# Two rows per partition, 64x64 tiles and a ScalarE that copies: a batched product with residual rebuilt around 8 KB runs

## The chip, the cores and the metric

The kernel runs on one core of one Trainium2 chip. The metric is the device time of one execution in microseconds (us), as the median of the runs. Before the change it is 322.92 us, the median of 3 runs between 322.70 and 323.04.

## The reference

128 batch items `x[b]` of 128 rows by 1024 float32 (64 MB in all), an index `subjects[b]` of 0 to 7 for each, and eight 128x128 weights:

```
w = weights[subjects]                        # (128, 128, 128)
out = x + einsum('bct,bcd->bdt', x, w)       # out[b] = x[b] + w[b].T @ x[b]
```

All of x is read once and all of the output, of the same size, is written once: 134 MB through the DMA engines, in float32.

## The kernel before, in words

The 128 items are worked in 32 turns of four (`NT = 32`, `G = H = 2`). A turn's four items lie in one of 12 slots of an SBUF buffer, `x_all`, with a row of an item on each partition: 4 KB in one run per item and partition. The product is added to the item in place, and the slot is stored from there.

- **Loads** (L134, issued at L223 to L224): ScalarE does nothing else. It issues 128 loads of 512 KB. Up to the twelfth turn nothing but the queue holds them up (slot 11 first waits until the weights that pass through it are sorted); after that the load of turn i waits until the store of turn i - 12 has landed (L222). In DRAM a load is read as 32 rows of 16 KB (`ROWS = 4`), in SBUF it is written as 128 runs of 4 KB.
- **Weights** (L192 to L239): one load on SP's queue, two transposes and twelve copies on VectorE and four copies on GpSimd put the eight matrices into `w_all`. Before each half turn VectorE copies two of them, picked by the index, into the `ws` buffers (`place`, L163).
- **Products** (`multiply`, L168): TensorE makes two matmuls of 128x128 by 512 columns for an item, eight in a turn, four for each half of the eight PSUM banks. The three matmuls at L200 on zeros come ahead of all.
- **Adds** (`add`, L183): VectorE adds half a turn, 128 x 2048, from PSUM to the items in their slot.
- **Stores** (L142, issued at L247 to L255): SP waits for the adds and stores a turn (2 MB), or two turns (4 MB) at a time for the last twelve. From the eighth turn on it holds a store back by four turns (`BEHIND`), and ceases to do so for the last eight. In SBUF a store reads runs of 16 KB (32 KB in the last six turns), in DRAM it writes rows of 4 KB.

The engines run from their own instruction streams, with semaphores between them. GpSimd only turns landed loads into a count that TensorE waits on (L240 to L245).

Of the kernel before, what the change touches and what calls it, by code (L numbers as in the profile page):

```python
# [25 lines left out]
F32 = mybir.dt.float32  # L26
I32 = mybir.dt.int32
ALU = mybir.AluOpType


G = 2
H = 2

N = 512

SLOTS = 12

P_SLOTS = 2

BEHIND = 4  # L40

EARLY = 8
LAST = 8

PAIR = 2
WHOLE = 6

DMA = 16

SORTED = 18  # L50

IDLE = 3

ROWS = 4

ALIGN = 4096
QUEUES = {mybir.EngineType.SP: "qSPDynamicHW", mybir.EngineType.Activation: "qActDynamicHW"}
# [23 lines left out]
def kernel(  # L81
# [7 lines left out]
    nc = tc.nc  # L89
    B, C, T = x.shape  # L90
    S, _, D = weights.shape
    NT = B // (G * H)

    def sbuf(name, *shape, dtype=F32):
        return ctx.enter_context(nc.sbuf_tensor(name, list(shape), dtype)).ap()


    room = -(nc.sbuf_base + -nc.sbuf_base % 32) % ALIGN
    if room:
        sbuf("room", C, room // 4)  # L100
    x_all = sbuf("x_all", C, SLOTS * H * G * T)
    xs = [
        x_all[:, i * H * G * T : (i + 1) * H * G * T].rearrange("c (q t) -> c q t", t=T)
        for i in range(SLOTS)
    ]
    w_all = sbuf("w_all", C, S, D)
    w_raw, w_mid, w_late = (xs[SLOTS - 1][:, q, :] for q in range(3))
    ws = [sbuf(f"w{i}", C, 1, D) for i in range(H * G)]
    zeros = sbuf("zeros", C, N)
    given, near, wrap = (sbuf(name, 1, B, dtype=I32) for name in ("given", "near", "wrap"))  # L110
    index = sbuf("index", 1, B + H * G, dtype=I32)
    ps = [
        ctx.enter_context(nc.psum_tensor(f"ps{i}", [D, G, T], F32)).ap() for i in range(P_SLOTS)
    ]
# [5 lines left out]
    s_product = tc.alloc_semaphore("s_product")  # L120
    s_added = tc.alloc_semaphore("s_added")

    s_ready = tc.alloc_semaphore("s_ready")
    s_go = tc.alloc_semaphore("s_go")

    s_slot = [tc.alloc_semaphore(f"s_slot{k}") for k in range(SLOTS)]
    s_head = tc.alloc_semaphore("s_head")
    s_sort = tc.alloc_semaphore("s_sort")

    def emptied(i):  # L130
        turns = i // SLOTS
        return DMA * (H * G + 1) * turns - (DMA * G if i >= SLOTS and i % SLOTS == 0 else 0)

    def load(engine, i, q):  # L134
        transfer(
            nc,
            engine,
            xs[i % SLOTS][:, q, :],
            x[i * H * G + q].rearrange("(a r) t -> a (r t)", r=ROWS),
        ).then_inc(s_head if i * H * G + q < G else s_slot[i % SLOTS], DMA)  # L140

    def store(i, n):  # L142
        at = i % SLOTS * H * G * T
        return transfer(
            nc,
            nc.sync,
            out[i * H * G : (i + n) * H * G].rearrange("g d t -> d g t"),
            x_all[:, at : at + n * H * G * T].rearrange(
                "d (o t) -> d o t", o=1 if i >= NT - WHOLE else n
            ),  # L150
        )

    def subjects_of(i):
        _, subject = nc.values_load_multi_w_load_instructions(
            index[0:1, i] if isinstance(i, slice) else index[0:1, bass.ds(i * (H * G), H * G)],
            engines=[mybir.EngineType.DVE],
            min_val=0,
            max_val=S - 1,
            skip_runtime_bounds_check_because="the index is clamped on the chip above",
        )  # L160
        return subject

    def place(h, subject):  # L163
        for q in range(h * G, (h + 1) * G):
            copy = nc.vector.tensor_copy(ws[q], w_all[:, bass.ds(subject[q], 1), :])  # L165
        copy.then_inc(s_go, 1)

    def multiply(slot, h):  # L168
        nc.tensor.wait_ge(s_go, 1).then_inc(s_go, -1)
        nc.tensor.wait_ge(s_ready, 1).then_inc(s_ready, -1)  # L170
        for q in range(h * G, (h + 1) * G):
            for t in range(0, T, N):
                at = slot * (H * G * T) + (q * T + t)
                mm = nc.tensor.matmul(  # L174
                    ps[h][:, q % G, t : t + N],
                    ws[q][:, 0, :],
                    x_all[:, bass.ds(at, N)],
                    start=True,
                    stop=True,
                )  # L180
        mm.then_inc(s_product, 1)

    def add(slot, h):  # L183
        mine = x_all[:, bass.ds(slot * (H * G * T) + h * G * T, G * T)]
        nc.vector.wait_ge(s_product, 1).then_inc(s_product, -1)  # L185
        nc.vector.tensor_tensor(  # L186
            mine, ps[h].rearrange("d g t -> d (g t)"), mine, ALU.add
        ).then_inc(s_added, 1)

    with tc.tile_critical():  # L190

        nc.sync.dma_start(  # L192
            w_raw, weights.rearrange("s (u j) d -> (s u) (j d)", j=S)
        ).then_inc(s_wall, DMA)
        nc.sync.dma_start(given, subjects.rearrange("(o b) -> o b", o=1)).then_inc(s_given, DMA)

        nc.vector.memset(zeros, 0.0).then_inc(s_zeros, 1)  # L197
        nc.tensor.wait_ge(s_zeros, 1)
        for _ in range(IDLE):
            nc.tensor.matmul(  # L200
                ps[P_SLOTS - 1][:, G - 1, :N], zeros[:, :D], zeros, start=True, stop=True
            )

        nc.vector.wait_ge(s_wall, DMA)
        nc.vector.transpose(  # L208
            w_mid.rearrange("p (e h w j) -> p j h e w", e=S, h=4, w=4), w_raw
        ).then_inc(s_sort, 1)  # L210
        nc.vector.memset(index[:, B:], 0).then_inc(s_index, 1)  # L211
        nc.vector.wait_ge(s_given, DMA)
        nc.vector.tensor_scalar(near, given, -S, S - 1, ALU.max, ALU.min).then_inc(s_index, 1)  # L213
        nc.vector.wait_ge(s_index, 2)
        nc.vector.tensor_scalar(wrap, near, 0, S, ALU.is_lt, ALU.mult).then_inc(s_index, 1)  # L215
        nc.vector.wait_ge(s_index, 3)
        nc.vector.tensor_tensor(index[:, :B], near, wrap, ALU.add).then_inc(s_index, 1)  # L217
        for i in range(NT):
            if i == SLOTS - 1:
                nc.scalar.wait_ge(s_sort, SORTED)  # L220
            if i >= SLOTS:
                nc.scalar.wait_ge(s_slot[i % SLOTS], emptied(i))  # L222
            for q in range(H * G):  # L223
                load(nc.scalar, i, q)  # L224

        nc.vector.wait_ge(s_sort, 1)
        nc.vector.transpose(w_late, w_mid).then_inc(s_sort, 1)  # L227

        def sort(engine, o, v):
            engine.tensor_copy(  # L230
                w_all[32 * v : 32 * (v + 1), 2 * o : 2 * (o + 1), :],
                w_late[32 * o : 32 * (o + 1)].rearrange("c (e v d) -> c v e d", v=4, d=D)[:, v],
            ).then_inc(s_sort, 1)

        nc.vector.wait_ge(s_sort, 2)
        nc.gpsimd.wait_ge(s_sort, 2)
        for o in range(4):
            for v in range(4):
                sort(nc.gpsimd if v == 3 else nc.vector, o, v)  # L239
        for i in range(NT):  # L240
            if i == 0:
                nc.gpsimd.wait_ge(s_head, DMA * G).then_inc(s_ready, 1)
                nc.gpsimd.wait_ge(s_slot[0], DMA * G).then_inc(s_ready, 1)
            else:
                nc.gpsimd.wait_ge(s_slot[i % SLOTS], emptied(i) + DMA * H * G).then_inc(s_ready, H)  # L245

        for i in [*range(NT - SLOTS), *range(NT - SLOTS, NT, PAIR)]:  # L247
            n = 1 if i < NT - SLOTS else PAIR
            nc.sync.wait_ge(s_added, (i + n + (BEHIND if EARLY <= i < NT - LAST else 0)) * H)
            if i == 0:  # L250
                nc.sync.dma_start(
                    out[: H * G].rearrange("g d t -> d g t"), xs[0]
                ).then_inc(s_slot[0], DMA)
            elif i + n < NT:
                store(i, n).then_inc(s_slot[i % SLOTS], DMA)  # L255


        nc.vector.wait_ge(s_index, 4)
        nc.vector.wait_ge(s_sort, SORTED)
        subject = subjects_of(slice(0, H * G))  # L260
        for h in range(H):
            place(h, subject)
        with nc.vector.Fori(0, NT) as turn:  # L263
            subject = subjects_of(turn + 1)
            for h in range(H):
                add(turn % SLOTS, h)
                place(h, subject)
        with nc.tensor.Fori(0, NT) as turn:
            for h in range(H):
                multiply(turn % SLOTS, h)  # L270

    with tc.tile_critical() as waits:
        for i in range(NT - SLOTS, NT - PAIR, PAIR):
            nc.scalar.wait_ge(s_slot[i % SLOTS], emptied(i + SLOTS))
    last = store(NT - PAIR, PAIR)

    tc.add_manual_dep(
        last.ins,
# [31 lines left out]
```

## Time and profile before

| | |
|---|---|
| median of the runs | 322.92 us |
| span of the profiled execution (first to last instruction) | 320.9 us |
| rest of its time, taken as the median less the span | 2.0 us |
| moved by DMA | 134.76 MB in 10,803 packets, mean 420 GB/s over the span |
| busy: TensorE, weight loads, VectorE, GpSimd | 78%, 32%, 54%, 1% |
| mean granted clock of TensorE | 0.893 |

The profile gives the span of one execution and not that execution's own time, so what lies around the span is put at 2.0 us. "Share" of a DMA queue is the time that its packets took, as a share of 16 engines' time; the two data queues are q1 (SP's, stores mostly) and q10 (ScalarE's, loads). A packet is counted by the side that is read. A row of a window (`a:b`) counts what begins in it.

A float32 matmul of the program stands twice in the trace, as two weight loads and two matmuls, one behind the other: 512 rows for 256 matmuls. One such row is called a pass below.

### The profile page before, as it was taken

Reading aid. Unit: us, or ns where it says so; the run is one execution under the profiler, and the core shown is the slowest. Engines: PE = TensorE matmul, PEld = TensorE weight load, DVE = VectorE, ACT = ScalarE, POOL = GpSimd, SP = SyncE. Lnnn points to the kernel's source line nnn. Section 1 sums busy time; section 2 is a strip of 40 time slices with the busy share of each in tenths; the row PEclk is TensorE's granted clock in tenths of the full one; section 3 lists DMA queues with packets and bytes.
Section 4 is the critical chain, followed back from the end, with each engine's and each line's share of the span. In section 5 each row is a group of like instructions: output and inputs, shape, how many; then the busy total and the mean of one; then the engine's idle time right before and its main releaser. Section 6 shows DMA issues by size and latency. Waiting matters only on the chain. (4 is left out here: it accounts for less than half of the span.)

```text
span 320.9 us, 2386 instructions
## 1 busy us (share of the span) xinstructions
PE 248.9 (78%) x518; PEld 102.8 (32%) x518; DVE 172.6 (54%) x216; POOL 1.9 (1%) x8
## 2 busy tenths in 40 slices
PE   6199999999997699998498469988599957874000
PEld 2134444444433244443133224333244422331000
DVE  4636776777676167775435362675367745066000
POOL 0200000000000000000000000000000000000000
PEclk9679999999999599999789797999799989599555
DMA  7999999999999999999999999999999999999996
GB/s 294 425 425 412 426 423 432 429 423 425 425 425 425 425 424 425 425 429 425 429 435 431 427 427 429 425 425 425 425 425 425 425 425 425 427 427 455 429 445 274
DMA packets 10803, 134.76 MB, mean 420 GB/s; under 512 B 2481, under 2 KB 2482, under 8 KB 3122
## 3 DMA queue, kind: packets, MB, share of 16 engines
q1 hardware_dynamic: 4658, 67.64, 49.7%
q10 hardware_dynamic: 6144, 67.12, 49.6%
q14 instruction: 1, 0.01, 0.0%
HBM read 67.63 MB, written 67.11 MB: 420 GB/s over the span
## 5 line engine op out<-in xcount | busy, mean ns | idle before, releaser
L174 PE MATMUL ps<-x_all,w 128*128 x512 | 243.8, 635 | 42.0 <-PEq L170 34.3
L186 DVE TENSOR_TENSOR x_all<-ps,x_all 128x2048 f32 x64 | 146.7, 2292 | 117.3 <-DVEq L185 117.3
L174 PEld LDWEIGHTS ps<-x_all,w 128*128 128x128 f32 x512 | 100.9, 203 | 185.2 <-issue 184.6
L165 DVE COPY w<-w_all 128x128 f32 x132 | 23.2, 219 | 0.8 <-DVE w_all L230 0.8
L200 PE MATMUL ps<-zeros 128*128 128x512 f32 x6 | 5.2, 1033 | 1.7 <-DVE zeros L197 1.7
L230 DVE COPY w_all<-x_all 32x256 f32<-32x256 f32 x12 | 3.9, 326 | 0.4
L208 DVE STREAM_TRANSPOSE x_all<-x_all 128x1024 f32<-128x1024 f32 x1 | 2.0, 1992 | 3.1 <-DMA x_all<-in_L_cond_weights_dram 3.1
L200 PEld LDWEIGHTS ps<-zeros 128*128 128x128 f32 x6 | 1.8, 328 | 3.7 <-issue 2.1
L230 POOL COPY w_all<-x_all 32x256 f32<-32x256 f32 x4 | 1.7, 425 | 8.3 <-DVE x_all L227 8.1
L227 DVE STREAM_TRANSPOSE x_all<-x_all 128x1024 f32<-128x1024 f32 x1 | 1.2, 1225 | 0.0
L197 DVE MEMSET zeros<- 128x512 f32 x1 | 0.5, 485 | 1.0 <-SPq L190 1.0
L217 DVE CUSTOM_DVE_ANT_0 index<-near,wrap 1x256 uint16<-1x256 uint16 x1 | 0.3, 280 | 0.0
L215 DVE TENSOR_SCALAR wrap<-near 1x128 int32<-1x128 int32 x1 | 0.2, 215 | 0.0
L213 DVE TENSOR_SCALAR near<-given 1x128 int32<-1x128 int32 x1 | 0.2, 205 | 0.0
L297 POOL MEMSET const-bfloat16-1.0<- 128x1 bf16 x1 | 0.1, 100 | 0.0
L297 POOL MEMSET const-float32-0.0<- 128x1 f32 x1 | 0.1, 98 | 0.2 <-issue 0.2
L297 POOL MEMSET const-uint8-127<- 128x1 uint8 x1 | 0.1, 98 | 0.0
L297 POOL MEMSET const-float32-1.0<- 128x1 f32 x1 | 0.1, 97 | 0.0
L297 DVE BASE_LOAD x1 | 0.0, 21 | 0.1
L211 DVE MEMSET index<- 1x4 int32 x1 | 0.1, 62 | 0.0
## 6 DMA issues: line engine op xcount, KB each, us to landing
x_all<-in_x_dram ACTq DMA_DIRECT2D x128, 512.0 KB, 34.2
out_dram<-x_all SPq DMA_DIRECT2D x20, 2048.0 KB, 18.3
out_dram<-x_all SPq DMA_DIRECT2D x6, 4096.0 KB, 30.3
x_all<-in_L_cond_weights_dram SPq DMA_DIRECT2D x1, 512.0 KB, 3.7
given<-in_itok_B_dram SPq DMA_DIRECT2D x1, 0.5 KB
```

The source lines that it names most:

```text
L165: copy = nc.vector.tensor_copy(ws[q], w_all[:, bass.ds(subject[q], 1), :])
L174: mm = nc.tensor.matmul(ps[h][:, q % G, t : t + N], ws[q][:, 0, :], x_all[:, bass.ds(at, N)], start=True, stop=True,)
L186: nc.vector.tensor_tensor(mine, ps[h].rearrange("d g t -> d (g t)"), mine, ALU.add).then_inc(s_added, 1)
L197: nc.vector.memset(zeros, 0.0).then_inc(s_zeros, 1)
L200: nc.tensor.matmul(ps[P_SLOTS - 1][:, G - 1, :N], zeros[:, :D], zeros, start=True, stop=True)
L208: nc.vector.transpose(w_mid.rearrange("p (e h w j) -> p j h e w", e=S, h=4, w=4), w_raw).then_inc(s_sort, 1)
L213: nc.vector.tensor_scalar(near, given, -S, S - 1, ALU.max, ALU.min).then_inc(s_index, 1)
L215: nc.vector.tensor_scalar(wrap, near, 0, S, ALU.is_lt, ALU.mult).then_inc(s_index, 1)
L217: nc.vector.tensor_tensor(index[:, :B], near, wrap, ALU.add).then_inc(s_index, 1)
L227: nc.vector.transpose(w_late, w_mid).then_inc(s_sort, 1)
L230: engine.tensor_copy(w_all[32 * v : 32 * (v + 1), 2 * o : 2 * (o + 1), :], w_late[32 * o : 32 * (o + 1)].rearrange("c (e v d) -> c v e d", ...
L297: nc = _bacc.Bacc("TRN2", target_bir_lowering=False, num_devices=1)
```

## The change

The work is still 32 turns of four items, but:

- **Layout.** Two rows of an item lie on one partition, so an item fills 64 partitions with runs of 8 KB, and a pair of items (`H = 2`) fills 128. A turn is two such pairs (`P = 2`). Loads are 1 MB, 64 in all, read as 32 rows of 32 KB and written as 128 runs of 8 KB. Stores write runs of 8 KB.
- **Two buffers.** Input has 4 slots (`x_in`), output 8 (`x_out`), instead of 12 that serve as both.
- **Products.** An item's contraction is split into the two rows of a partition (`R = 2`, summed in PSUM), and its output rows too, so an item takes 8 matmuls of 64x64 by 512 columns: 32 in a turn, 1024 in all. The first pair of a turn uses the diagonal tiles of the array (rows and columns 0 to 63, or 64 to 127, for its items); the second pair uses the other two tiles, so that its items come out in each other's half of the partitions.
- **Residual.** Ones are added to the weights' diagonal when they are placed (`same`), so the matmul's result is the output, and only a copy out of PSUM is left. VectorE places 64x256 pieces, four in a turn, into one of two sets of buffers, for the turn after next.
- **Copies.** VectorE copies the first pair, two copies of 128x1024 in a turn. ScalarE copies the second pair, four copies of 64x1024, and puts each into the other half of the partitions (`swap`). A ScalarE copy of one element then tells SP.
- **Loads in ScalarE's loop.** ScalarE issues the first eight loads at once and the weights behind the first; the loads of turn i + 4 follow in its stream on its copies of turn i and on VectorE's signal `s_eaten`.
- **Weights.** They come in rows of 512 bytes on ScalarE's queue, are spread over the partitions by four matmuls with a 0/1 matrix (`pick`), and are copied out of PSUM by ScalarE and VectorE, one half each. Six matmuls on zeros come first.
- **Stores.** One turn each for 20 turns, then pairs of turns; none is held back.

On ScalarE's stream, the loads before stand one behind the other, with waits for slots only; `x_all` is the slot buffer, `in_x_dram` the input:

```order
L67 DMA x_all<-in_x_dram 128x1024 x44
L67 DMA x_all<-in_x_dram 128x1024 [waits s_sort]
L67 DMA x_all<-in_x_dram 128x1024 x3
L67 DMA x_all<-in_x_dram 128x1024 [waits s_slot0]
L67 DMA x_all<-in_x_dram 128x1024 x3
```

After the change the stream begins with nine loads (`in_L_cond_weights_dram` are the weights), and then goes through turns such as this one (`s_product1` comes from TensorE, `s_room1` from landed stores):

```order
L63 DMA x_in<-in_x_dram 128x2048
L63 DMA x_out<-in_L_cond_weights_dram 128x8x128
L63 DMA x_in<-in_x_dram 128x2048 x7
L231 ACT_TABLE_LOAD
L231 COPY w_all<-ps 128x8x128 [waits s_picked]
L306 UNCONDITIONAL_BRANCH
L225 ISA [waits s_room1,s_product1]
L225 COPY x_out<-ps 64x1024
```

```order
L225 ISA [waits s_product1]
L225 COPY x_out<-ps 64x1024
L225 ISA
L225 COPY x_out<-ps 64x1024
L243 ISA
L243 COPY mark<-same 1x1
L61 ISA [waits s_eaten]
L63 DMA x_in<-in_x_dram 128x2048
L61 ISA
L63 DMA x_in<-in_x_dram 128x2048
```

So the 48 loads of the first twelve turns stood ahead of any wait for a store, and now eight stand ahead of the first wait for a product.

On TensorE, the loop before has two waits in a turn, each ahead of four matmuls (`s_go` is for placed weights, `s_ready` for landed loads):

```order
L174 ISA [waits s_go,s_ready]
L174 MATMUL ps<-x_all,w 128x512
L174 ISA
L174 MATMUL ps<-x_all,w 128x512
L174 ISA
L174 MATMUL ps<-x_all,w 128x512
```

Now a turn has 32 matmuls of half the partitions, and waits besides for the banks that the copies have freed (`s_free0` from VectorE, `s_free1` from ScalarE):

```order
L202 MATMUL ps<-x_in,w 64x512 [waits s_go,s_ready,s_free0,s_free1]
L202 MATMUL ps<-x_in,w 64x512 x7
L202 MATMUL ps<-x_in,w 64x512 [waits s_free0,s_free1]
L202 MATMUL ps<-x_in,w 64x512 x23
```

Eight matmuls fill the first half of the banks, and the wait for the second half stands between them and the other 24.

The core of the diff:

```diff
+    def load(k, p, turn=None):
+        at = (k % IN * P + p) * SIZE
...
+            x_in[:, at : at + SIZE],
+            x[bass.ds(first, H)].rearrange("h (b r) t -> (h b) (r t)", r=ROWS),
+        ).then_inc(s_in[k % IN], DMA)
...
+            out[i * Q : (i + n) * Q].rearrange("(g h) (a r) t -> (h a) g (r t)", h=H, r=R),
+            x_out[:, at : at + n * P * SIZE].rearrange("a (o f) -> a o f", o=1),
...
+        for b in range(BANKS):
+            if b < BANKS // 2:
+                for p in range(P):
+                    nc.tensor.wait_ge(s_free[p], 1 + p).then_inc(s_free[p], -1 - p)
+            for r in range(R):
+                for p in reversed(range(P)):
+                    for h in range(H):
+                        bank = b * 2 % BANKS + (b * 2 // BANKS + h) % 2
+                        e, t = divmod(bank * N, T)
+                        rows = slice(h * A, (h + 1) * A)
+                        cols = slice((h ^ p) * A, ((h ^ p) + 1) * A)
+                        at = (i % IN * P + p) * SIZE + r * T + t
+                        mm = nc.tensor.matmul(
+                            ps[p][cols, bank],
+                            ws[i % 2][p][rows, 0, r * D + e * A : r * D + (e + 1) * A],
+                            x_in[rows, at : at + N],
...
+                        if r == R - 1 and b >= BANKS // 2:
+                            mm.then_inc(s_product[p], 1)
...
+    def swap(slot, half, h):
+        at, banks = half_of(slot, half)
+        return nc.scalar.copy(
+            x_out[h * A : (h + 1) * A, bass.ds(at + SIZE, T)],
+            ps[1][(1 - h) * A : (2 - h) * A, banks].rearrange("d b n -> d (b n)"),
+        )
...
+    def take(i):
+        slot = i % OUT if isinstance(i, int) else i
+        nc.scalar.wait_ge(s_room[1], 1).then_inc(s_room[1], -1)
+        for half in range(2):
+            nc.scalar.wait_ge(s_product[1], H).then_inc(s_product[1], -H)
+            for h in range(H):
+                swap(slot, half, h).then_inc(s_free[1], 1)
+        nc.scalar.copy(mark[:, bass.ds(slot, 1)], same[:1, 0, :1]).then_inc(s_added[1], 1)
...
+        with nc.scalar.Fori(0, NT // IN - 1) as turn:
+            for k in range(IN):
+                take((turn * IN + k) % OUT)
+                nc.scalar.wait_ge(s_eaten, 1).then_inc(s_eaten, -1)
+                for p in range(P):
+                    load(IN + k, p, turn)
```

The four products of a bank order `b`, with `r` fixed, go to the four tiles of the array in the order second pair (both items), first pair (both items). Products of the first half of the banks are done after three quarters of a turn's matmuls, those of the second half at its end.

More of the change, by code (lines that the diff above doesn't have):

```diff
@@ L161, in subjects_of, with place @@
         return subject
[L163 to L168, printed above, removed]
+    def place(u, subject):
+        return [
+            nc.vector.tensor_tensor(
+                ws[u][p][h * A : (h + 1) * A],
+                w_all[h * A : (h + 1) * A, bass.ds(subject[p * H + h], 1), :],
+                same[h * A : (h + 1) * A],
+                ALU.add,
+            )
+            for p in range(P)
+            for h in range(H)
+        ]
@@ L169, in multiply @@
+    def multiply(i):
         nc.tensor.wait_ge(s_go, 1).then_inc(s_go, -1)
         nc.tensor.wait_ge(s_ready, 1).then_inc(s_ready, -1)
[L171 to L180, printed above, removed]
@@ L194 @@
+    with tc.tile_critical():
+        load(0, 0)
+        transfer(
+            nc,
+            nc.scalar,
+            w_raw.rearrange("c (s d) -> c s d", s=S),
+            weights.rearrange("s c d -> c s d"),
         ).then_inc(s_wall, DMA)
@@ L259 @@
[L259 to L270, printed above, removed]
+            if i - OUT in stored:
+                n, count = stored[i - OUT]
+                for p in range(P):
+                    nc.gpsimd.wait_ge(s_out[i % OUT], count).then_inc(s_room[p], n)
@@ new lines @@
+            nc.gpsimd.wait_ge(s_in[i % IN], DMA * P * (i // IN + 1)).then_inc(s_ready, 1)
+        for i, n in stores[:-1]:
+            for p in range(P):
+                nc.sync.wait_ge(s_added[p], i + n)
+            store(i, n).then_inc(s_out[i % OUT], DMA)
+        nc.vector.wait_ge(s_index, 4)
+        subject = subjects_of(slice(0, 2 * Q))
+        nc.vector.wait_ge(s_picked, S * D // N * R)
+        sort(nc.vector.tensor_copy, 0)
+        nc.vector.wait_ge(s_sort, R)
+        nc.vector.wait_ge(s_same, H)
@@ L272 @@
+        with nc.tensor.Fori(0, NT // IN):
+            for i in range(IN):
+                multiply(i)
     with tc.tile_critical() as waits:
[L273 to L275 removed]
+        for i, n in stores[:-1]:
+            if i >= NT - OUT:
+                nc.scalar.wait_ge(s_out[i % OUT], stored[i][1])
+    last = store(*stores[-1])
     tc.add_manual_dep(
```

222 lines of the change are left out of this document (130 added, 92 removed).

## The prediction

> **What bounds the kernel now.** I read the page's parts 1 to 3 first: engines, the span in slices, queues.
>
> ```profile
> PE 248.9 (78%) x518; PEld 102.8 (32%) x518; DVE 172.6 (54%) x216; POOL 1.9 (1%) x8
> PE   6199999999997699998498469988599957874000
> DMA  7999999999999999999999999999999999999996
> DMA packets 10803, 134.76 MB, mean 420 GB/s; under 512 B 2481, under 2 KB 2482, under 8 KB 3122
> q1 hardware_dynamic: 4658, 67.64, 49.7%
> q10 hardware_dynamic: 6144, 67.12, 49.6%
> ```
>
> The DMA engines are full in every slice but the first and the last, and the packets of both queues take 99.3% of the span. TensorE ends three slices before the end and loses nothing by its gaps. The windows of busy time say how even the rate is.
>
> ```profile
> 0.00:2.00 2.00, 0.34 (x1) 0.34 (x2) 0.51 (x2) 0.20 (x4) 1.00 0.00 0
> 100.00:200.00 100.00, 80.19 (x163) 32.98 (x162) 52.26 (x61) 0.00 (x0) 0.90 1.01 427
> 300.00:317.00 17.00, 0.00 (x0) 0.00 (x0) 0.00 (x0) 0.00 (x0) 0.50 1.00 426
> ```
>
> Nothing flows for the first 2 us. Then the rate (last column, GB/s) is the same when loads and stores mix (427) and when stores run alone (426). So the time is 2.0 us of start, the bytes at some 425 GB/s, and an end. Only two things can change it: what a byte costs on the DMA engines, and holes in their work.
>
> **What a packet costs.** The DMA view, taken by windows, prices packets by size. These are 30 to 48 us (q1 sends only 4 KB packets, the first store), 60 to 290 us (q10 sends 16 KB reads and its completions) and 300.5 to 309 us (q1 sends 32 KB reads and one completion):
>
> ```profile
> q10 hardware_dynamic: 501, 5.55, 73.8%
> q1 hardware_dynamic: 485, 1.99, 26.8%
> ```
> ```profile
> q10 hardware_dynamic: 4406, 48.08, 49.5%
> ```
> ```profile
> DMA packets 113, 3.67 MB, mean 432 GB/s; under 512 B 1, under 2 KB 1, under 8 KB 1
> q1 hardware_dynamic: 113, 3.67, 101.1%
> ```
>
> A 4 KB packet takes 0.268 x 18 us x 16 / 485 = 159 ns, a 32 KB one 1.011 x 8.5 x 16 / 112 = 1228 ns. The line through both is 152.7 ns for each 4 KB and 6.4 ns for each packet. By it a 16 KB packet takes 617 ns; 48.08 MB are 2935 of them, and the 1821.6 us of the middle row leave 6.9 ns for each of the other 1471, the completions. In all three rows the side that is written takes pieces of 4 KB, so a written piece's own price, if it has one, hides in the 152.7 ns.
>
> **The change, term by term. Packets.** Read pieces: before, 4096 for loads, 4096 for stores, 128 for weights; after, 2048, 3328 and 1024 (the weights come in 512-byte rows). That is 1920 fewer x 6.4 ns / 16 engines = 0.8 us. Completions: 16 for each transfer, about 1010 fewer x 6.9 / 16 = 0.4 us. Written pieces: 134.2 MB in 4 KB are 32,768, in 8 KB 16,384, so 1024 fewer on each engine. No row shows 8 KB pieces written. From below such a piece costs nothing; from above as much as a read one, 6.4 ns: 0 to 6.6 us. I take half, 3.3 us, because no row is nearer to one end. Sum: 4.5 us saved, from 1.2 to 7.8.
>
> The Trainium skill ("DMA: Bandwidth & Descriptors", section "Why small descriptors are slow") states about 3 cycles of overhead for each packet inside the DMA engine; with its clock of 850 MHz my estimate by that page is 3.5 ns for a piece, 3.6 us in place of the 3.3. No run here shows it yet.
>
> **The hole at the start.** This is the term against the change. Before, the loads ran far ahead:
>
> ```profile
> 0.90 23.58 ACTq L67 DMA_DIRECT2D x_all<-in_x_dram  x31
> 14.54 9.84 PE L174 MATMUL ps<-x_all,w 128*128 x16 [7.71 <-DVE w L165]
> 18.11 0.33 PEld L174 LDWEIGHTS ps<-x_all,w 128*128 128x128 f32 x1 [0.52 <-issue]
> 18.96 0.33 PEld L174 LDWEIGHTS ps<-x_all,w 128*128 128x128 f32 x1 [0.52 <-issue]
> 20.35 0.19 PEld L174 LDWEIGHTS ps<-x_all,w 128*128 128x128 f32 x1 [0.24 <-issue]
> 20.78 0.19 PEld L174 LDWEIGHTS ps<-x_all,w 128*128 128x128 f32 x1 [0.24 <-issue]
> ```
> ```profile
> 14.00:20.00 6.00, 5.46 (x7) 2.35 (x8) 0.26 (x2) 0.00 (x0) 0.50 1.01 429
> 20.00:24.00 4.00, 4.00 (x11) 1.63 (x9) 2.56 (x3) 0.00 (x0) 1.00 1.01 426
> ```
> ```profile
> DMA packets 771, 8.24 MB, mean 429 GB/s; under 512 B 255, under 2 KB 256, under 8 KB 272
> ```
>
> 31 loads, 16 MB, were issued by 24.5 us. Now 8 MB and the weights stand ahead of the first wait. At the 429 GB/s of loads alone (3.8 to 23 us, last row) 8.91 MB take 20.8 us, the small weight rows 0.4 more: the engines run dry at 2.0 + 21.2 = 23.2 us. Work for them comes only when turn 0 has been copied out. When is that?
>
> ```profile
> 1.67 5.16 PE L200 MATMUL ps<-zeros 128*128 128x512 f32 x6 [1.67 <-DVE zeros L197]
> L186 DVE TENSOR_TENSOR x_all<-ps,x_all 128x2048 f32 x64 | 146.7, 2292 | 117.3 <-DVEq L185 117.3
> L165 DVE COPY w<-w_all 128x128 f32 x132 | 23.2, 219 | 0.8 <-DVE w_all L230 0.8
> 285.44 7.13 PE L174 MATMUL ps<-x_all,w 128*128 x16 [1.74 <-PEq L170]
> ```
>
> A pass starts every 0.86 us at a granted clock of 0.50 and every 0.43 at 1.00 (the two windows above), which came 5.8 us after the start of turn 0 (20.35 less 14.54). Six matmuls on zeros are 12 passes from 1.67: if the clock rises as it did there, 6.8 passes in 5.8 us and 5.2 in 2.2, to 9.7. The weights land ahead of that (2.0 + 2.5 for the load before them + 1.6). Spreading them is four matmuls, 8 passes, 3.4 us: 13.1. The copy out of PSUM is half of L186's elements, 1.15 us: 14.3. Four placings at some 0.3 us (L165's 219 ns has half the elements): 15.5. Turn 0, with four tiles abreast, is 16 pass times, 7.13 us as in the row of a warm turn: 22.7. ScalarE has no copy in this trace. Two copies of 1024 at L186's rate are 2.3 us for half a turn: the first half's products are ready at three quarters, 20.9, copied at 23.2; the second's at 25.5. With the mark, some 0.2 us, the next load and store are issued at 25.8 and flow 1.1 us later (SP's first issue was at 0.96, the first bytes at 2.0): 26.9. The hole is 3.8 us. Its bounds: TensorE starts turn 0 at the 14.5 of before and ScalarE needs 0.7 us a copy, 1.2 us; the spreading runs at the clock of 0.50, 3.4 us later, with 0.6 for GpSimd's 0/1 matrices, 7.8.
>
> **The turns after that.** A turn is 4.19 MB, 9.8 us at 428 GB/s. TensorE, four abreast, needs 7.1 us, and waits some 0.8 for ScalarE's halves (2.3 us of copies beside 1.8 us of matmuls): 8 us. ScalarE: four copies, the mark, two issues at 0.6 or so, 6 us. VectorE: two copies and four placings, 3.5 us. So all fit with 1.8 us to spare, and the new waits of ScalarE, behind which the loads are queued, are covered by three turns of loads in flight; if TensorE took over 9.8 us this cover would be gone, and each turn would cost the excess.
>
> **The end.** In the 30 to 48 us rows the queues shared the engines by packet size, 26.8 to 73.8. Loads of 32 KB packets against stores of 16 KB will take about two thirds while both have work, so loads keep ahead, stores pile up in the eight output slots, and the end is stores alone, as now. I cost it at nothing. If the stores did not pile up, the last turn's 7 us of products and 2.3 of copies would show, less what is left of the pair before: up to 7 us.
>
> What goes at no price: VectorE's adds (L186) and the held-back stores, which the full DMA engines hide.
>
> **Sum.** Against the span: 320.9 - 4.5 + 3.8 = 320.2; with the same 2.0 us around it as before 322.2, against the median of 322.92. A measurement of this kernel can tell some 0.2%, 0.65 us, so this is at the edge of it.
>
> **The rivals.**
>
> *A, the change pays more fully.* Written pieces cost as much as read ones, or the hole closes to its lower bound: 322.9 - 7.8 + 3.8 = 318.9, or 322.9 - 4.5 + 1.2 = 319.6; both, 316.3. For it: no row excludes either. Against it: a 32 KB packet with eight written pieces would then spend 51 of its 1228 ns on them.
>
> *B, no gain, only the hole.* Written pieces cost nothing: 322.9 - 1.2 + 3.8 = 325.5; with the hole at its upper bound 329.5. Also here: the stores don't pile up. For it: 16 KB and 32 KB reads gave the same 426 GB/s.
>
> *C, slower: the tiles don't run four abreast.* A program matmul is two passes on the same tile. If passes start strictly in order, the second pass of a tile waits 0.43 us for the first, and the three other tiles' matmuls wait behind it. Then one matmul begins every 0.43 us, 13.8 us for a turn of 32, and TensorE is the bound: 15.6 + 32 x 13.8 + 16 (last copies, start of the store, 4 MB at 427 GB/s, end) = 473 us of span, 475. It decides as soon as fewer than 64 x 0.43 / 9.8 = 2.8 tiles are at work on average. For it: the weight loads come in order, two for each matmul, one for each pass. Against it: at the full clock a weight load runs beside the pass before it (20.35 and 20.78 above, 0.43 us apart with nothing added), so the engine does take work ahead of the running pass; nothing in this trace uses more than one tile. The Trainium skill ("TensorE: Matmul & The Clock Gate", "Part 3: Packing small matmuls", "The mechanism") states that matmuls start and end in program order, which would make it so, but also that matmuls on different tiles overlap; this trace can show neither.
>
> *D, slower: the weight loads.*
>
> ```profile
> L174 PEld LDWEIGHTS ps<-x_all,w x512: 186/190/338, 14.5 to 291.6; 128*128 128x128 f32 x171
> ```
>
> They now number 64 in a turn. One after the other at 190 ns they take 12.2 us, and the time is 15.6 + 32 x 12.2 + 16 = 422; at half the columns 95 ns, 6.1 us, hidden. The point is 153 ns. Between them lies a turn just over 9.8 us: 325 to 345.
>
> **How the numbers follow.** Forecast 0.47, own range 320.5 to 324.5; A 0.20; B 0.13; C 0.15; D 0.05. Of the forecast's 0.47, 0.22 lies under 322.3, 0.16 within 0.2% of 322.92, 0.09 above. Faster: 0.22 + 0.20 = 0.42. Same: 0.16. Slower: 0.09 + 0.13 + 0.15 + 0.05 = 0.42. The range leaves out C, most of D and the last of A, together 0.2: 318 to 330.
>
> **What would show it.** Right: windows of the steady part at 430 GB/s or a little over, 32 KB packets of q10 near 1215 ns, a hole of some 4 us in the DMA row at 23 to 27 us and none later, weight loads of four tiles within one pass time, TensorE done well before the last store. Wrong: 1228 ns a packet (B); a hole in a later slice; TensorE busy without gap to the end with a matmul every 0.43 us (C); weight loads back to back (D).

## The result

The changed kernel takes 332.52 us (median of 4 runs, 332.23 to 332.71) against 322.98 (4 runs, 322.70 to 323.12): a ratio of 1.0294, 95% interval 1.0279 to 1.0308. It is slower by 9.5 us. The forecast was 322.2 us, in a range of 318 to 330.

### The profile page after: what moved, and what is told of

It reads as the page before. It is cut to its first block, busy times and chain, and to the rows that moved or that the text cites. A ratio compares the mean times of both kernels' runs of the same rounds, so it can differ in the third digit from the quotient of the medians.

```text
span 330.9 us, 5722 instructions
## 1 busy us (share of the span) xinstructions
PE 255.5 (77%) x2068; PEld 93.3 (28%) x2068; DVE 138.0 (42%) x207; ACT 137.2 (41%) x162; POOL 1.6 (0%) x7
## 5 line engine op out<-in xcount | busy, mean ns | idle before, releaser
L202 PE MATMUL ps<-x_in,w 64*64 64x512 f32 x2048 | 244.2, 619 | 51.8 <-PEq L193 49.0
L225 ACT COPY x_out<-ps 64x1024 f32 (+1 forms) x128 | 128.8, 1007 | 161.9 <-ACTq L240 159.5
L202 PEld LDWEIGHTS ps<-x_in,w 64*64 64x64 f32 x2048 | 88.6, 138 | 207.3 <-issue 207.3
L219 DVE COPY x_out<-ps 128x1024 f32 x64 | 78.4, 1224 | 158.8 <-DVEq L351 158.8
L177 DVE TENSOR_TENSOR w<-w_all,same 64x256 f32<-64x256 f32 x136 | 57.1, 420 | 3.7
L259 PE MATMUL ps<-x_out 128*128 128x512 f32 x12 | 7.9, 825 | 1.7 <-DVE x_out L256 1.7
L243 ACT COPY mark<-same 1x1 f32 (+1 forms) x32 | 6.1, 190 | 0.8
L231 DVE COPY w_all<-ps 128x1024 f32<-128x1024 f32 x1 | 1.2, 1224 | 10.0 <-PE ps L296 10.0
L259 PEld LDWEIGHTS ps<-x_out 128*128 128x128 f32 x12 | 3.1, 270 | 5.6 <-issue 4.0
L296 PE MATMUL ps<-x_out 128*128 128x512 f32 x8 | 3.6, 592 | 0.0
L231 ACT COPY w_all<-ps 128x1024 f32<-128x1024 f32 x1 | 1.0, 1012 | 4.9 <-PE ps L296 4.9
L296 PEld LDWEIGHTS ps<-x_out 128*128 128x128 f32 x8 | 1.5, 190 | 1.9 <-issue 1.9
```

What stands on the lines that cost most here:

```text
L177: nc.vector.tensor_tensor(ws[u][p][h * A : (h + 1) * A], w_all[h * A : (h + 1) * A, bass.ds(subject[p * H + h], 1), :], same[h * A : (h + ...
L202: mm = nc.tensor.matmul(ps[p][cols, bank], ws[i % 2][p][rows, 0, r * D + e * A : r * D + (e + 1) * A], x_in[rows, at : at + N], start=r == ...
L219: return nc.vector.tensor_copy(x_out[:, bass.ds(at, T)], ps[0][:, banks].rearrange("d b n -> d (b n)"))
L225: return nc.scalar.copy(x_out[h * A : (h + 1) * A, bass.ds(at + SIZE, T)], ps[1][(1 - h) * A : (2 - h) * A, banks].rearrange("d b n -> d ( ...
L231: engine(w_all.rearrange("c s (r e a) -> c r s e a", r=R, e=R)[:, r], ps[0][:, r * R : (r + 1) * R].rearrange("c g (s a e) -> c (g s) e a" ...
L243: nc.scalar.copy(mark[:, bass.ds(slot, 1)], same[:1, 0, :1]).then_inc(s_added[1], 1)
```

## The profile after

The page of the changed kernel, in its parts 1 to 3:

```profile
span 330.9 us, 5722 instructions
PE 255.5 (77%) x2068; PEld 93.3 (28%) x2068; DVE 138.0 (42%) x207; ACT 137.2 (41%) x162; POOL 1.6 (0%) x7
DMA  7984999999999999999999999999999999999991
DMA packets 7863, 134.81 MB, mean 407 GB/s; under 512 B 1457, under 2 KB 2482, under 8 KB 2482
```

The row of the DMA engines was full from the second slice to the last but one. Now it has a dent in the fourth slice, at 24.8 to 33.1 us, and its last slice is nearly empty (1, where it was 6). The windows show both places in microseconds; the last three columns are the granted clock, the DMA share and GB/s.

```profile
16.00:22.00 6.00, 5.22 (x36) 2.14 (x40) 1.86 (x5) 0.00 (x0) 0.00 (x0) 0.72 1.02 437
22.00:24.00 2.00, 2.00 (x24) 0.84 (x20) 0.00 (x0) 0.00 (x0) 0.00 (x0) 1.00 0.61 262
24.00:26.00 2.00, 1.57 (x16) 0.36 (x8) 1.33 (x2) 1.85 (x2) 0.00 (x0) 1.00 0.00 0
26.00:28.00 2.00, 1.69 (x16) 0.60 (x16) 1.94 (x3) 1.95 (x3) 0.00 (x0) 1.00 0.00 0
28.00:30.00 2.00, 1.88 (x20) 0.78 (x20) 0.86 (x3) 0.42 (x2) 0.00 (x0) 1.00 0.49 106
30.00:32.00 2.00, 2.00 (x24) 0.90 (x20) 0.00 (x0) 0.00 (x0) 0.00 (x0) 1.00 1.24 410
32.00:34.00 2.00, 1.76 (x19) 0.38 (x11) 1.22 (x1) 1.68 (x2) 0.00 (x0) 1.00 0.77 279
...
100.00:200.00 100.00, 85.09 (x724) 30.78 (x723) 47.49 (x71) 48.28 (x58) 0.00 (x0) 0.97 1.01 430
...
318.00:322.00 4.00, 0.00 (x0) 0.00 (x0) 0.00 (x0) 0.00 (x0) 0.00 (x0) 0.50 0.95 410
322.00:326.00 4.00, 0.00 (x0) 0.00 (x0) 0.00 (x0) 0.00 (x0) 0.00 (x0) 0.50 0.44 188
326.00:331.00 5.00, 0.00 (x0) 0.00 (x0) 0.00 (x0) 0.00 (x0) 0.00 (x0) 0.50 0.03 13
```

**The hole.** The rows from 22 to 34 us hold 1.22 + 0 + 0 + 0.98 + 2.48 + 1.54 = 6.2 us of DMA work in 12 us: 5.8 us are lost. The timeline says what the engines waited for (start, duration, engine, line; in brackets the idle time before):

```profile
16.78 8.79 PE L202 MATMUL ps<-x_in,w 64*64 64x512 f32 x64 [3.77 <-PEq L193]
24.13 4.10 ACT L225 COPY x_out<-ps 64x1024 f32 x4 [10.07 <-ACTq L240]
28.23 0.49 ACTq L63 DMA_DIRECT2D x_in<-in_x_dram  x1
28.54 0.62 SPq L63 DMA_DIRECT2D out_dram<-x_out  x1
```

Turn 0 is multiplied from 16.78 to 25.57 us, ScalarE copies until 28.23, and only behind that stand the next load and the first store.

**The late end.** The first DMA engine has written its part of the last store at 323.50 us, the thirteenth at 324.13, the next two at 325.9, and the sixteenth at 329.45. Before, all sixteen ended between 318.79 and 319.57; its last packets begin in these rows (the last two columns are the DMA share and GB/s):

```profile
318.00:319.00 1.00, 0.00 (x0) 0.00 (x0) 0.00 (x0) 0.00 (x0) 0.50 0.24 98
319.00:320.00 1.00, 0.00 (x0) 0.00 (x0) 0.00 (x0) 0.00 (x0) 0.50 0.00 0
```

What starts from 324.5 to 330 us in the changed kernel:

```profile
DMA packets 9, 0.20 MB, mean 36 GB/s; under 512 B 3, under 2 KB 3, under 8 KB 3
```

Six data packets of 32 KB and three completions, while most engines are empty. The share of 0.03 in the row 326 to 331 is one engine in sixteen at work for the first part of it. This lag is 5.95 us, against 0.78 before; at the end of the kernel it lengthens the time by all of its 5.2 us more.

**The packets.** From 313 to 322 us only paired stores run, whose packets are read in 32 KB and written in pieces of 8 KB:

```profile
DMA packets 130, 3.74 MB, mean 415 GB/s; under 512 B 16, under 2 KB 16, under 8 KB 16
q1 hardware_dynamic: 130, 3.74, 96.5%
```

0.965 x 9 us x 16, less 16 completions of 9 ns, over 114 packets is 1218 ns, where 4 KB pieces gave 1228. Over the whole execution the packets take 317.4 us of each engine on the mean, against 319.0: 1.6 us gained.

So the span, longer by 10.0 us, has +5.8 (hole), +5.2 (late engine) and -1.6 (packets); 0.6 us I can't place.

## The experiments

The question was which of the two losses is real and of what kind. The theories, as the expectations name them: theory 1, the late engine is the one that fetches TensorE's instructions; theory 2, it falls behind when the flow restarts after the hole; theory 3, it is slowed in proportion to the number of TensorE's instructions; and later theory S, the two queues share the engines by packet size, and so decide what is left for the end. The rival of all of them is that the hole alone, or slower products, cost the time. "Rows" are TensorE's matmul rows on the page, and "lag" is the time from the first to the last DMA engine at the end of the last store, from the trace.

**The hole made longer.** `idle_12` puts six more matmuls on zeros ahead of all:

```diff
-IDLE = 6
+IDLE = 12
```

> Twelve matmuls on zeros ahead of the products in place of six: 12 more passes of 0.43 us, so turn 0 and with it the first wait of the loads is 5.2 us later. If the hole at the start is paid in full, 337.7 us with a hole of 11 us; if later slack hides it, 332.5 us. The tail should stay at 6 us by theory 1; by theory 2 (restart after the hole) too, or a little more.

Measured: 337.23 us, ratio 1.0478 (1.0412 to 1.0543), 4.7 us over the changed kernel. The windows of `idle_12`:

```profile
24.00:26.00 2.00, 2.00 (x16) 0.78 (x12) 0.00 (x0) 0.00 (x0) 0.00 (x0) 0.59 0.00 0
...
30.00:32.00 2.00, 1.32 (x13) 0.60 (x16) 1.67 (x3) 1.95 (x3) 0.00 (x0) 1.00 0.00 0
32.00:34.00 2.00, 1.89 (x20) 0.60 (x16) 1.23 (x3) 0.79 (x2) 0.00 (x0) 1.00 0.30 66
```

The first packet after the hole starts at 33.87 us instead of 29.51: 4.4 us more hole, 4.7 us more time. The hole is paid about one to one; nothing behind it makes it good.

**The hole closed by trading slots.** `in8_out4` gives eight slots to the input and four to the output, in the same memory:

```diff
-IN = 4
+IN = 8
-OUT = 8
+OUT = 4
```

> Eight input slots and four output slots in place of 4 and 8 (the loop of TensorE then holds 8 turns, not 4). 16 MB of loads stand ahead of the first wait, so the hole at 24 to 30 us should close: 5.7 us less. Theory 1 (the late last engine comes from instruction fetches, which take time on single DMA engines): the longer loop fetches more, so the tail after most engines have ended stays at 6 us or grows to 8; 326.5 to 329 us. Theory 2 (the late engine comes from the restart after the hole and from loads that wait for their turn): the tail goes with the hole, to about 1 us; 321 to 323 us. If the hole were not what costs the time, the time stays at 332.5 us.

Measured: 352.55 us, ratio 1.0889 (1.0849 to 1.0929). Windows of `in8_out4`:

```profile
20.00:36.00 16.00, 14.70 (x124) 5.15 (x120) 6.33 (x8) 7.06 (x8) 0.00 (x0) 0.92 1.01 420
280.00:291.00 11.00, 10.20 (x92) 3.62 (x88) 6.41 (x11) 5.92 (x8) 0.00 (x0) 1.00 0.04 15
301.00:307.00 6.00, 5.31 (x48) 1.75 (x44) 4.12 (x6) 4.21 (x5) 0.00 (x0) 1.00 0.00 0
```

The hole at 24 us is gone (first row, share 1.01), but the end has four holes, of which two are shown, and all three forecasts, 332.5 us at most, missed. With four output slots and stores of two turns, a pair of turns can't be computed before the pair ahead of it is out, so TensorE and the stores take turns. `in8_out4_single` has the same slots and stores one turn at a time:

```diff
-PAIR = 2
+PAIR = 1
```

> Eight input and four output slots as in in8_out4, but every store is one turn (PAIR = 1), so that the last eight turns no longer wait for a store of two turns. The hole at the start is closed (5.7 us) and the four holes at the end of in8_out4 go. If the late last engine is a thing of its own (one DMA engine whose packets are slowed a little while the engines compute), the tail of 4 to 6 us stays: 326 to 328 us. If the tail belongs to the hole or to the paired stores: 321 to 323 us.

Measured: 340.93 us, ratio 1.0575 (1.0538 to 1.0611).

```profile
20.00:36.00 16.00, 14.70 (x128) 5.23 (x124) 6.72 (x9) 7.45 (x9) 0.00 (x0) 0.95 1.02 417
290.00:320.00 30.00, 27.36 (x248) 9.88 (x239) 15.25 (x21) 16.20 (x19) 0.00 (x0) 1.00 0.65 275
```

Again no hole at the start. From 290 us on TensorE is busy (27.36 of 30 us) and the DMA share 0.65: the end is bound by the products of one turn in 8 us, since all loads had landed at 277 us (at 290 in the changed kernel). Both forecasts missed here too. But the store that the first engine ends at 287.6 us is ended by the last one at 293.0: 5.4 us late, with no hole at the start. Theory 2 falls, so far as it needs the hole.

**Instruction fetch.** `pe_loop_8` makes the body of TensorE's loop eight turns instead of four, `pe_unrolled` does without the loop:

```diff
-        with nc.tensor.Fori(0, NT // IN):
-            for i in range(IN):
+        with nc.tensor.Fori(0, NT // (2 * IN)):
+            for i in range(2 * IN):
```

> Only the loop of TensorE is changed: 8 turns are written out in its body in place of 4, run 4 times in place of 8. Theory 1 (instruction fetches make one DMA engine late): two or more further fetch packets, the last engine is 1 to 3 us later, 333.5 to 335.5 us. Theory 2 (restart after the hole): no change, 332.5 us.

```diff
-        with nc.tensor.Fori(0, NT // IN):
-            for i in range(IN):
-                multiply(i)
+        for i in range(NT):
+            multiply(i)
```

> TensorE's loop is written out in full: 32 turns, 1024 matmuls, no loop. Theory 1: many more fetch packets, at 0.7 to 2 us each on an engine; if they fall on one engine, over 8 us more, 340 us and up; if they spread, less. Theory 2: no change, 332.5 us.

Measured: 332.68 us, 1.0316 (1.0285 to 1.0347), lag 5.73 us; and 333.58 us, 1.0325 (1.0302 to 1.0349), lag 6.42. In `pe_unrolled` the queue of instruction fetches moved 0.28 MB, against 0.03 in the changed kernel:

```profile
q8 instruction: 17, 0.28, 0.3%
```

Fetching ten times as much changed the time by 1 us and spread over several engines: half of them ended some 3 us late, the last one hardly later than without.

The trace settles it. It doesn't name the engine of a packet, but while the engines are full a packet begins 3 to 4 ns before the end of the one ahead of it on its engine, so from each engine's last packet the chain can be followed back, here to 52 us. In `pe_unrolled` the fetches behind that point lie on nine other engines and none on the last. In the changed kernel the last engine has no fetch either. It has 144 packets that took over 8 ns more than the median of their size and queue, mostly 10 to 90 ns more, 5.4 us in sum; none of the other fifteen has more than seven such packets. Theory 1 falls for this engine.

**The number of instructions.** `after_n256` and `before_n256` make each matmul in two of 256 columns, in the changed kernel and in the one before; the products are the same. In `before_n256`:

```diff
-            for t in range(0, T, N):
+            for t in range(0, T, N // 2):
...
-                    ps[h][:, q % G, t : t + N],
+                    ps[h][:, q % G, t : t + N // 2],
```

> Each 64x64 matmul of 512 columns is made as two of 256: twice the matmuls and weight loads on TensorE, the same products and the same transfers. Theory 3 (one DMA engine is slowed in proportion to the instructions that run): the last engine is twice as late, 10 to 12 us after the rest in place of 6, 337 to 339 us. If the number of instructions does not matter: 332.5 us with the same tail; if TensorE's turn grows over 9.8 us by weight loads, holes between the turns show that.

> The kernel before the change with each matmul of 512 columns made as two of 256: 1024 passes in place of 512, nothing else. Theory 3: the last engine is 1.2 to 3 us after the rest in place of 0.6; 324 to 325 us. If the number of instructions does not matter: 323 us.

Measured: 337.41 us, 1.0448 (1.0431 to 1.0465), and 324.24 us, 1.0037 (1.0023 to 1.0052). TensorE's busy time did not change with twice the rows:

```profile
L203 PE MATMUL ps<-x_in,w 64*64 64x256 f32 x4096 | 244.8, 391 | 55.4 <-PEq L193 51.3 <-ACT x_out L226 1.6
```

It was 244.2 us for 2048 rows (below). The windows of `after_n256`:

```profile
314.00:318.00 4.00, 0.00 (x0) 0.00 (x0) 2.48 (x5) 1.90 (x3) 0.00 (x0) 0.94 0.08 33
...
328.00:334.00 6.00, 0.00 (x0) 0.00 (x0) 0.00 (x0) 0.00 (x0) 0.00 (x0) 0.50 0.06 27
```

0.06 is one engine in sixteen, for 6 us at the very end, and about as much at 314 to 318 us, where the other engines had no store left until the last copies ended. The last store but one was ended by the first engine at 313.45 us and by the last one 11.1 us later; during the gap the late engine caught up in part, and its lag at the last store is 6.50 us. The rest of the 4.9 us lies ahead of that: the last copies ended at 315.7 us, 4.3 us later than in the changed kernel. That they came late because a slot is free only when the slowest engine has written its store fits the program, but no run tests it. Theory 3 forecast the time and the 11 us; the other two give no reason for them.

`half_products` goes the other way. It leaves the products of r = 1 out, so half of the contraction is not computed:

```diff
-            for r in range(R):
+            for r in range(1):
...
-                            start=r == 0,
-                            stop=r == R - 1,
+                            start=True,
+                            stop=True,
...
```

> The changed kernel without the products of the second row of a partition (r = 1): half the contraction is left out, half the matmuls, the same transfers and copies. Turn 0 is 3.5 us shorter, and the hole with it. Theory 3: the tail falls from 6 us to about 3; 326 us. If the number of instructions does not matter, the tail stays at 6 us: 329 us.

Measured: 326.80 us, 1.0126 (1.0099 to 1.0153). Both losses shrink: turn 0 is shorter, so the engines are empty only from 24.1 to 25.9 us, where the next packet starts: 1.8 us, against 5.4 taken in the same way in the changed kernel. The lag is 3.87. If the two losses are the whole cause, the time is 332.5 - (5.4 - 1.8) - (5.95 - 3.87) = 326.8 us; with the hole taken up to the median engine's first packet (6.0 against 1.9 us) it is 326.3. The measurement agrees.

Is it TensorE's instructions, or anybody's? `before_gpsimd_992` adds to the kernel before 31 one-element writes of GpSimd in each turn, into unused SBUF:

```diff
...
+            for k in range(i * 31, i * 31 + 31):
+                nc.gpsimd.memset(spare[k % 4 * 32 : k % 4 * 32 + 1, k // 4 : k // 4 + 1], 0.0)
```

> The kernel before, with 31 one-element writes of GpSimd added in each turn, 992 in all, to SBUF that nothing reads; TensorE's 518 rows in the trace stay as they are. Theory 3 in the form that any engine's instructions slow the one DMA engine, at the 2.5 ns for each row that the TensorE runs gave: the last DMA engine ends 3 us behind the others and the time is 325 to 325.6 us. Theory 3 in the form that only TensorE's instructions do it: 0.8 us behind, 323.0 us.

Measured: 326.01 us, 1.0085 (1.0069 to 1.0102), slower by 2.8 us. The writes themselves move no data through DMA and nobody waits for them:

```profile
L247 POOL MEMSET room<- 1x1 f32 x992 | 92.0, 93 | 192.5 <-DMA x_all<-in_x_dram 156.4
```
```profile
319.00:320.00 1.00, 0.00 (x0) 0.00 (x0) 0.00 (x0) 0.00 (x0) 0.50 0.08 33
320.00:321.00 1.00, 0.00 (x0) 0.00 (x0) 0.00 (x0) 0.00 (x0) 0.50 0.15 66
321.00:322.00 1.00, 0.00 (x0) 0.00 (x0) 0.00 (x0) 0.00 (x0) 0.50 0.08 33
```

These are the last microseconds of its DMA, where two engines and then one go on alone. The lag of 3.71 us is near the 3 us that theory 3 in its wider form (any engine's instructions) forecast, but two causes are in it. The 992 writes are written out without a loop and have to be fetched. The queue of fetches in `before_gpsimd_992`, and then in the kernel before:

```profile
q14 instruction: 9, 0.07, 0.1%
```
```profile
q14 instruction: 1, 0.01, 0.0%
```

Each such fetch takes 309 ns. Followed back to 52 us, the chain of the last engine, which ends at 322.77 us, holds six of the seven fetches behind that point, 1.9 us, and only six slow packets. So the last engine is late by theory 1. The other one, which ends at 321.24 us, has no fetch and 71 slow packets, 1.8 us in sum: this is the effect of theory 3, and this engine ends 1.7 us later than the last engine of the kernel before. All runs that show the lag at the end, with the slow packets of the one engine that has them, counted from 52 us on:

| kernel | TensorE rows | all instructions | lag, us | slow packets | their excess, us |
|---|---|---|---|---|---|
| before | 518 | 2386 | 0.78 | 21 | 0.4 |
| `before_gpsimd_992` | 518 | 3378 | 3.71 (fetches), 2.18 (slow packets) | 71 | 1.8 |
| `before_n256` | 1030 | 3666 | 2.33 | 104 | 1.8 |
| `half_products` | 1044 | 3674 | 3.87 | 105 | 3.2 |
| `pe_unrolled` | 2068 | 5705 | 6.42 | 155 | 5.8 |
| `pe_loop_8` | 2068 | 5714 | 5.73 | 148 | 5.6 |
| after | 2068 | 5722 | 5.95 | 144 | 5.4 |
| `idle_12` | 2080 | 5746 | 6.43 | 154 | 5.6 |
| `after_n256` | 4116 | 9818 | 11.1, then 6.50 | 217 | 10.1 |

Between kernels that differ in nothing else, an added row of TensorE (with its weight load) adds 2.1 to 2.8 ns of excess to the one engine; an added GpSimd write adds 1.4 ns. Across different kernels the count of rows alone does not give the lag: `before_n256` and `half_products` have nearly the same and differ by 1.5 us. The slow packets are of both queues; in the changed kernel the last one begins at 313.6 us, and the last copy ended at 311.7. What an instruction sends to that engine, the runs don't say, and no run tried to take it away. One candidate is the record that is kept of each instruction for the profile: all runs on record have a span and a granted clock taken from such records, so there is no time of an execution without them, and the theory is shown for recorded executions alone. The medians of the runs move by the same amounts as the profiled executions.

**What the end hangs on.** The last question was why trading slots made things worse. `after_rows4` reads the loads in rows of 16 KB, and changes nothing else; `in8_out4_rows4` does it to `in8_out4_single`:

```diff
-ROWS = 8
+ROWS = 4
```

> The changed kernel with its loads read in rows of 16 KB instead of 32 KB; nothing else. Theory S: the prediction's step that loads keep ahead and stores pile up hangs on the packet sizes (32 against 16 KB); with equal sizes each queue gets half, stores do not pile up in the eight output slots, and the end shows the last turns' products: 336 to 342 us. Rival (the sizes of the packets set no share): only 2048 more read pieces, 0.8 us: 333.3 us.

> Eight input slots, four output slots, stores of one turn, and loads read in rows of 16 KB instead of 32 KB, so that loads and stores send packets of one size. Theory S (the queues share the DMA engines by packet size, and with the 32 KB loads this is what starved the stores in in8_out4_single): no hole at the start, loads no longer run eight turns ahead, no holes at the end; the late DMA engine stays at some 5 to 6 us, since the TensorE work is that of the changed kernel. 332.5 less the 5.6 of the hole plus 0.8 for 2048 more read pieces: 326 to 328 us. Rival (in8_out4_single was slow for its four output slots, whatever the packets): holes of some 3 us in each of the last six turns, 337 to 341 us.

Measured: 341.20 us, 1.0563 (1.0534 to 1.0592), and 332.62 us, 1.0303 (1.0258 to 1.0348). Packets, MB and share of the two queues from 40 to 70 us, in the changed kernel and then in `after_rows4`:

```profile
q10 hardware_dynamic: 352, 7.86, 61.1%
q1 hardware_dynamic: 354, 5.01, 39.2%
```
```profile
q1 hardware_dynamic: 460, 6.64, 51.8%
q10 hardware_dynamic: 460, 6.21, 48.6%
```

The queues send equal numbers of packets (4-byte completions counted), 352 and 354, or 460 and 460, so the queue with the longer packets gets the more time. The Trainium skill ("DMA: Bandwidth & Descriptors", section "Queues, rings and completion order") says that an engine goes round between its queues packet by packet. The counts agree, with every single piece that the trace lists as a packet taken as a turn. With 32 KB packets the loads of the changed kernel land at 290 us and stores fill the rest; with 16 KB they land at 311, and the last turns' products lie bare. Windows of `after_rows4`:

```profile
316.00:327.00 11.00, 6.45 (x60) 2.24 (x52) 5.91 (x11) 5.42 (x8) 0.00 (x0) 1.00 0.02 6
327.00:338.00 11.00, 0.00 (x0) 0.00 (x0) 0.00 (x0) 0.00 (x0) 0.00 (x0) 0.52 0.89 381
```

11 us without DMA, then the last pair's store. Theory S is right there. For `in8_out4_rows4` it expected 326 to 328 us, and that missed: the six holes of `in8_out4_single` shrink to two, of 4.4 and 3.8 us, but its loads land at 309 us, and the last two turns follow with too few stores to cover them.

```profile
310.00:315.00 5.00, 4.36 (x40) 1.75 (x44) 2.91 (x5) 2.58 (x4) 0.00 (x0) 1.00 0.29 125
...
320.00:325.00 5.00, 0.00 (x0) 0.00 (x0) 1.25 (x3) 0.65 (x2) 0.00 (x0) 0.77 0.49 210
```

Early loads leave work for TensorE at the end, late loads leave too few stores, and four output slots hold too few in both cases. `in8_out4_rows4_half` is the same kernel with r = 1 left out (half of the contraction is not computed):

> The kernel of in8_out4_rows4 with the products of r = 1 left out (half of the contraction is not computed), 1044 rows of TensorE in place of 2068. Theory 3 (the late engine goes with the number of TensorE rows): the last DMA engine ends some 3.9 us late in place of 6, and the time is 2 us under that of in8_out4_rows4, 324 to 326 us. Rival (the late engine comes from the two buffers, from ScalarE's loop or from the hole): no difference from in8_out4_rows4.

Measured: 330.66 us, 1.0226 (1.0203 to 1.0249), 2.0 us less, the difference that theory 3 gave, but above its 324 to 326 us. It proves little: the holes at its end are there still, and they, not the late engine, end it (the lag at its last store is 0.14 us).

No version beats the kernel before. Without its hole, at the same end, the changed kernel would take about 332.5 - 5.8 = 326.7 us (an estimate from its own windows), and no trade of the slots that was tried gets there.

## Why the prediction was wrong, point by point

**Where it failed: "The end ... I cost it at nothing."** The stores did pile up, and the end is stores alone, as the step said: the last copies end at 312 us, and 318 to 322 us runs at 410 GB/s. But the end is not "as now". One engine is 5.95 us behind, because the change turned 518 rows of TensorE into 2068. The prediction read the sixteen DMA engines as one resource with a rate; the store is done when the slowest of them is, and the trace of before had the seed of it, a lag of 0.78 us. 5.2 us are missing in the sum for this, and no rival had it. What such an instruction does to the engine stays open. With the two terms below, which were sized wrongly, 5.2 + 2.0 + 2.9 = 10.1 of the 10.3 us between forecast and measurement are placed.

**Mis-sized: the hole, 3.8 us forecast, 5.8 measured,** inside its bounds of 1.2 to 7.8. Up to the weights' copy out of PSUM, at 14.3 us, the times came out as forecast. The four placings then took 0.44 us each, not 0.3, so that turn 0 began at 16.78 us instead of 15.5, and it took 8.79 instead of 7.13: it was priced as a warm turn, but TensorE had been idle for 3.77 us ahead of it, and the granted clock was 0.72 in 16 to 22 us. So the copies ended at 28.2 instead of 25.5, and packets flowed from 29.5 to 30.2 on, engine by engine, where 26.9 was forecast. The engines ran dry 0.9 us later than worked out, at 24.1. The rule that the hole is paid in full was right (`idle_12`).

**Mis-sized: the packets, 4.5 us forecast, 1.6 measured.** A written piece costs 2.25 ns: a 32 KB store fell from 1228 to 1219 ns with four pieces fewer. That is 2.3 us, not 3.3, inside the bounds. By the Trainium skill ("DMA: Bandwidth & Descriptors", section "Why small descriptors are slow") the estimate was 3.5 ns; the measurement decides. A read piece costs 4 ns rather than 6.4 (two 16 KB stores of before, 616 ns each, against one of 32 KB). The weights in rows of 512 bytes cost 1024 x 27 ns / 16 = 1.7 us against 1.3 for 128 rows of 4 KB, and were priced at 6.4 ns a row, as pieces beside whole packets. Slow packets where the flow starts again, between 29 and 52 us, take 1.4 us of each engine, where the kernel before had 0.5 there.

**Right: the turns, and so C and D false.** The groups of the changed kernel:

```profile
L202 PE MATMUL ps<-x_in,w 64*64 64x512 f32 x2048 | 244.2, 619 | 51.8 <-PEq L193 49.0
L225 ACT COPY x_out<-ps 64x1024 f32 (+1 forms) x128 | 128.8, 1007 | 161.9 <-ACTq L240 159.5
L202 PEld LDWEIGHTS ps<-x_in,w 64*64 64x64 f32 x2048 | 88.6, 138 | 207.3 <-issue 207.3
L219 DVE COPY x_out<-ps 128x1024 f32 x64 | 78.4, 1224 | 158.8 <-DVEq L351 158.8
L177 DVE TENSOR_TENSOR w<-w_all,same 64x256 f32<-64x256 f32 x136 | 57.1, 420 | 3.7
```

64 passes of a warm turn take 7.44 us, 0.116 us each where a pass alone takes 0.43: the tiles run four abreast. Four weight loads, 138 ns on the mean, go within one pass time. Of the two statements of the Trainium skill on this ("TensorE: Matmul & The Clock Gate", "Part 3: Packing small matmuls", "The mechanism"), the trace agrees with the one by which tiles overlap. C took the one on program order to hold up the other tiles, at 475 us, and they are not held up; whether matmuls still end in program order, the trace, where their ends are modelled, doesn't show. A copy of ScalarE takes 1.01 us (taken as 1.15), and a turn has room to spare, since 100 to 200 us runs at 430 GB/s.

**The rivals.** B, "no gain, only the hole", came nearest: 325.5 us, or 329.5 with the hole at its upper bound. It had the sign and not the second cause. The range ended at 330 since no case added 5 us at the end: the "up to 7 us" for stores that don't pile up stood in the text and was named under B, but in none of B's times.

## What to carry to other kernels

When all time is DMA time, look at the sixteen engines one by one at the end of the last transfer: a change that multiplies small instructions can make one of them late by microseconds, with the mean rate as good as before. Before a lag is put down to a cause, look at what the late engine carried: in `before_gpsimd_992` the lag had the forecast size and another cause. Price the first turn at the clock and with the waits that it will have, not as a warm one, and count what is left to transfer until the first result is out. Splitting a pool of slots that served input and output in turn takes from both ends: the loads' lead at the start, or the stores' pile at the end.

## What the runs showed of the hardware

- In recorded executions one DMA engine of the sixteen has slow packets that add up to 2.1 to 2.8 ns for each added TensorE row (`before_n256`, `half_products`, `after_n256`), and to 1.4 ns for each added GpSimd write.
- 992 GpSimd writes of one element, written out without a loop, made a kernel slower by 2.8 us: their fetches, 309 ns for each 8 KB, came mostly to one DMA engine.
- Two queues with work share the engines by equal numbers of packets: 32 KB against 16 KB gave 61.1% and 39.2%, one size 48.6% and 51.8%.
- A written piece costs 2.25 ns and a read one 4 ns inside a packet stream; a packet of 512 bytes takes 27 ns.
- Two 256-column matmuls in place of one of 512 left TensorE's busy time as it was, 244.8 against 244.2 us, with 64x64 tiles.
